# Later stores, later second row loads, an earlier gates' pool and a reordered last output in a graph layer of 32 batches

## The chip, the core and the metric

One Trainium2 chip, one core. Times are device microseconds of that core. A trace is one execution; a median is over 4 executions where no number is told.

## The reference, cut to what matters

```python
h = relu(layernorm(x))                              # x: (32, 512, 256) float32
# branch 1: convolution over the 512 positions
c = relu(bn1(conv1x1(h.T)));  c = bn2(conv17(c));  x_conv = relu(c + h.T).T
# branch 2: graph messages
s = h @ w_se.T + b_se                               # 3 features
A = exp(-|s_n - s_m|^2) * adj                       # (512, 512) for each batch
x_nmp = A @ relu(h @ w_msg.T + b_msg)
# gates
gi = [x_conv, x_nmp] @ w_ih.T + b_ih;  gh = h @ w_hh.T + b_hh
r = sigmoid(gi_r + gh_r);  z = sigmoid(gi_z + gh_z);  n = tanh(gi_n + r * gh_n)
out = x + (1 - z) * n + z * h
```

## The kernel before

TensorE does everything that is a product. The 17-tap convolution is 25 smaller products for each of seven groups of positions (175 in all), with additions on VectorE before (`x`, `xd`, `w`) and after (`z`, `y`). Five streams of work (rows, begins, graphs, conv, gates) are woven into one instruction order at build time: the program keeps a guessed clock `now` and guessed free times of VectorE and ScalarE, and each stream yields the time at which it may go on. Nothing of this is decided on the chip. There, each engine has its own list. In the trace before, a GpSimd store whose data was ready at 256.29 us left only at 260.12, behind a row's store for which GpSimd had stood 3.56 us.

A normalised and transposed row (512 KB) is `HT`. It is stored to DRAM (`hd`) and read back up to three times: as `hT` for the first convolution, as `hTg` for the messages, as `hTb` for the gates. The graph sums go out as `nd` and come back as `xnb`. The partial outputs of the convolution go out as `cd` and come back as `xconv`. GpSimd issues most stores, SyncE most loads.

```python
    def load_row(b):
        if b not in HR:
            HR[b] = front.tile([P, ND, N], F32, name="hT", bufs=2)
            nc.sync.dma_start(HR[b], HD[b])
            HR_AT[b] = now + 8.0

    def load_sums(b, d):                       # called behind the last product of gates(b - 1)
        if b < B and (b, d) not in XN:
            XN[b, d] = late.tile([P, N], F32, name="xnb", bufs=2)
            nc.sync.dma_start(XN[b, d], ND_[b, d])
# ... evacuate(): one partial output of the convolution
        part = late.tile([P, Q * U], F32, name="part", bufs=3)[:, : Q * (last - first)]
        act.activation(part..., y..., AF.Identity, bias=..., scale=...)
        act.free += 0.7
        PARTS.append(act.free + 4.0)           # the third next may not start before this
        later(act.free + 0.4, lambda: nc.gpsimd.dma_start(CD[b][:, o, n0:n1], part[:, : n1 - n0]))
# ... begin(b), the later rows (b >= 8): transposed by VectorE
            HT[b] = front.tile([P, ND, N], F32, name="hT", bufs=2)
            turning = True
            for o in range(ND):
                dve.transpose(HT[b][:, o, :], xb[:, o, :])
                if o < ND - 1:
                    yield dve.free
            nc.gpsimd.dma_start(HD[b], HT[b])
            begun, turning = b + 1, False
# ... all_rows()
                rows_wait = True
                for k in (b, b + 1):
                    if k in batches(g) and k < begun:
                        load_row(k)
                yield HR_AT[b]
                yield from rows(g, b)
# ... the convolution, from the 25th product on: a third weight is made from the two loaded
                if m == 24:
                    late_pools()               # loads whh and wih of the gates
                yield lambda: len(X2) > m and len(WS) > m
                if 25 <= m + 1 < 50 and W_AT[m + 1] <= now:
                    third_weight(m + 1)        # VectorE: w[:, 2] = w[:, 0] + w[:, 1]
# ... the streams: generator, guessed length, start
        "gates": (all_gates(), 31.25 * PER, 1.6),
```

## Time and profile before

| | us |
|---|---|
| time, median of 4 runs (range) | 2126.8 (2125.6 to 2129.2) |
| span of the profiled run | 2124.6 |
| TensorE busy | 2064.3 |
| of it lost to half clock | 21.1 |
| idle between the first and the last matmul | 49.4 |
| after the last matmul | 9.1 |

How to read it: busy, idle, 1.8 us of start-up and the end make the span. "Lost to half clock" is worked out: the busy time inside the trace's half-clock periods (granted clock 0.50 to 0.51), times one half. The lines behind these numbers stand in the prediction.

### The profile page before, as it was taken

To read this page: it belongs to the slowest core of one execution; us is meant where nothing else is said; L and a number is where in the kernel's file an instruction comes from. 1 tells how busy PE (TensorE), PEld (TensorE's weight loads), DVE (VectorE), ACT (ScalarE), POOL (GpSimd) and SP (SyncE) were. 2 spreads that over 40 slices of the span, in tenths; PEclk is the share of its full clock that TensorE was granted. 3 is DMA by queue.
4 is the path that set the end of the run, shared out by engine and by line. 5 is a ranking of instruction groups with operands and counts; after the bars stand their busy time and mean duration, and the time that the engine had idled before them with its cause. 6 is when DMAs were issued, how large, how long until landed. Compare 5 with 4: busy or idle time off the path is not lost. (4 is left out here: it accounts for less than half of the span.)

```text
span 2124.6 us, 25898 instructions
## 1 busy us (share of the span) xinstructions
PE 2064.3 (97%) x8756; PEld 1266.6 (60%) x8756; DVE 1511.3 (71%) x2660; ACT 756.9 (36%) x1267; POOL 339.9 (16%) x582
## 2 busy tenths in 40 slices
PE   9999899999999999999999999999999999999998
PEld 6887666655665555655566655556655566654443
DVE  6887779878874686875687857568876778863333
ACT  5555343235333235323353223443143522233111
POOL 2000212112111112110121111221111201112111
PEclk9999999999999999999999999999999999999999
DMA  7446778777766758676576775676876756624332
GB/s 282 169 145 205 248 240 217 199 205 208 215 180 200 188 140 226 186 204 188 152 218 177 198 203 164 181 190 192 224 193 168 203 165 161 171 57 134 85 93 40
DMA packets 546436, 383.07 MB, mean 180 GB/s; under 512 B 456576, under 2 KB 473472, under 8 KB 545664
## 3 DMA queue, kind: packets, MB, share of 16 engines
q1 hardware_dynamic: 512992, 282.17, 50.2%
q0 software_dynamic: 28624, 86.01, 11.8%
q10 hardware_dynamic: 4688, 13.24, 1.6%
q8 instruction: 70, 1.15, 0.2%
q14 instruction: 62, 0.51, 0.1%
HBM read 281.95 MB, written 99.35 MB: 179 GB/s over the span
## 5 line engine op out<-in xcount | busy, mean ns | idle before, releaser
L136 PE MATMUL ps_acc<-xnb,wih 128*128 128x512 f32 (+1 forms) x772 | 364.0, 594 | 2.5 <-DMA xnb<-nd 2.5
L136 PE MATMUL ps_acc<-xconv,wih 128*128 128x512 f32 (+1 forms) x772 | 363.2, 593 | 0.0
L136 PE MATMUL ps_acc<-hTb,whh 128*128 128x512 f32 x768 | 358.3, 596 | 4.5 <-DMA hTb<-hd 2.8
L136 PEld LDWEIGHTS ps_c<-xd,w 128*128 128x128 f32 x2400 | 294.0, 191 | 30.1 <-issue 24.7
L136 PE MATMUL ps_c<-xd,w 128*128 128x135 f32 (+1 forms) x2400 | 303.8, 279 | 1.0 <-DVE z L127 1.0
L1028 POOL DMA_DIRECT2D out_dram<-res x252 | 164.1, 657 | 610.7 <-DVE res L127 528.9
L136 PEld LDWEIGHTS ps_acc<-xnb,wih 128*128 128x128 f32 x772 | 143.5, 190 | 163.7 <-issue 154.7
L136 PEld LDWEIGHTS ps_acc<-xconv,wih 128*128 128x128 f32 x772 | 144.1, 191 | 158.2 <-issue 154.9
L136 PEld LDWEIGHTS ps_acc<-hTb,whh 128*128 128x128 f32 x768 | 141.7, 190 | 157.9 <-issue 147.2
L136 PE MATMUL ps_g<-at,msg 128*128 128x512 f32 x512 | 226.5, 593 | 0.6 <-DVE at L127 0.5
L136 PEld LDWEIGHTS ps_b<-x,w 128*128 128x128 f32 x1200 | 157.1, 191 | 50.9 <-issue 36.1
L136 PE MATMUL ps_b<-x,w 128*128 128x135 f32 (+1 forms) x1200 | 164.7, 280 | 8.1 <-ACT at L127 4.0
L127 DVE TENSOR_TENSOR r<-ps_acc,r 128x512 f32<-128x512 f32 (+1 forms) x65 | 44.3, 682 | 178.2 <-PE ps_acc L136 178.2
L127 ACT ACTIVATE mid<-ps_b 128x270 f32<-128x270 f32 (+1 forms) x150 | 59.5, 396 | 301.5 <-PE ps_b L136 293.8
L136 PEld LDWEIGHTS ps_g<-at,msg 128*128 128x128 f32 x512 | 95.8, 190 | 114.3 <-issue 111.5
L127 DVE TENSOR_TENSOR msg<-ps_g,bmsg 128x256 f32<-128x256 f32 x128 | 53.9, 422 | 137.6 <-PE ps_g L136 137.3
L136 PE MATMUL ps_g<-hT,w 128*128 128x512 f32 (+4 forms) x288 | 123.6, 579 | 23.2 <-DMA hT<-hd 23.2
L127 DVE SCALAR_TENSOR_TENSOR x<-x,x 128x544 f32<-128x544 f32 (+5 forms) x161 | 137.7, 855 | 2.7
L127 ACT ACTIVATE z<-ps_acc,brz 128x512 f32<-128x512 f32 x64 | 44.0, 687 | 248.5 <-PE ps_acc L136 235.3
L127 DVE TENSOR_TENSOR x<-x 128x272 f32<-128x272 f32 (+5 forms) x280 | 127.5, 500 | 0.3
L136 PE MATMUL ps_g<-wmsg,hTg 128*128 128x259 f32 x496 | 125.3, 384 | 0.3 <-DVE aug L127 0.3
L127 ACT ACTIVATE h<-ps_g,bn_shift,bn_scale 128x252 f32<-128x252 f32 (+4 forms) x208 | 85.4, 486 | 102.5 <-PE ps_g L136 101.9
(114 smaller groups left out, 2623.4 us busy)
## 6 DMA issues: line engine op xcount, KB each, us to landing
w<-wd SPq DMA_DIRECT2D x125, 768.0 KB, 5.4
m_sb<-in_adj_dram SPq DMA_DIRECT2D x384, 64.0 KB, 3.1
hd<-hT POOLq DMA_DIRECT2D x32, 512.0 KB, 6.0
hT<-hd SPq DMA_DIRECT2D x32, 512.0 KB, 4.2
hTb<-hd SPq DMA_DIRECT2D x32, 512.0 KB, 5.1
xnb<-nd SPq DMA_DIRECT2D x64, 256.0 KB, 3.2
xconv<-cd SPq DMA_DIRECT2D x32, 512.0 KB, 4.9
res<-in_x_dram SPq DMA_DIRECT2D x256, 64.0 KB, 2.8
```

The costliest lines, as they stand in the source:

```text
L127: getattr(self.engine, name)(*tiles, **more)
L136: nc.tensor.matmul(ps, lhsT, rhs, **more)
L1028: queue.dma_start(OB[b][:, s.start // 32 : s.stop // 32, o * P + 32 * g : o * P + 32 * g + 32], y[at, s].rearrange("i (k j) -> i k j", j=32),)
```

## The change

Its intent is to take waits from TensorE. It has six parts.

- **a, stores.** GpSimd's stores of rows and sums are put into its list when their data is expected, not at once, so that they don't hold up others.
- **b, rows.** A later row's store comes after both transposes; the second row is loaded 2.5 us after the first.
- **c, pool.** The gates' weights are loaded as soon as the 25 weights exist.
- **d, spacing.** Partial outputs 5 us apart instead of 4.
- **e, bank.** A product whose bank the exponentials hold is planned after them.
- **f, last output.** z times the old row is added before the last sum, the hidden state's product goes behind that of z, and the last sum is cut 384/128 instead of 256/256.

```diff
 # a
+    def store_at(t, dst, src):
+        todo = [lambda: nc.gpsimd.dma_start(dst, src)]
+        ...
+        STORES.append(run)
+        later(t, run)
+    def settle_stores():                       # called ahead of each new row tile and load
+        while STORES:
+            STORES.pop(0)()
-            nc.gpsimd.dma_start(HD[b], HT[b])
+            store_at(act.free + 0.4, HD[b], HT[b])
-        nc.gpsimd.dma_start(ND_[b, d], sums)
+        store_at(act.free + 0.4, ND_[b, d], sums)
 # b
             yield lambda: b not in NORMS
+            yield NORM_AT[b]
 ...
                 if o < ND - 1:
                     yield dve.free
+            yield dve.free + 0.4
             nc.gpsimd.dma_start(HD[b], HT[b])
 ...
-                for k in (b, b + 1):
-                    if k in batches(g) and k < begun:
-                        load_row(k)
+                load_row(b)
+                if b + 1 in batches(g) and b + 1 < begun:
+                    later(now + 2.5, lambda b=b: load_row(b + 1))
 # c
                 if m == 24:
+                    yield lambda: len(WS) >= 25
+                if late is None and len(WS) >= 25:
                     late_pools()
 # d
-        PARTS.append(act.free + 4.0)
+        PARTS.append(act.free + 5.0)
 # e
-                yield max(X_AT[m], W_AT[m])
+                yield max(X_AT[m], W_AT[m], bank_at if g > 0 else 0.0)
 # f
+            if is_last(o):
+                dve.tensor_tensor(z[:, s], z[:, s], r[:, s], op=ALU.mult)
+                dve.transpose(r[:, s], z[:, s])
+                dve.tensor_tensor(y[:, s], r[:, s], y[:, s], op=ALU.add)
 ...
+            dve.tensor_tensor(zh, z, hT[:, o, :], op=ALU.mult)            # mix_ahead
+            dve.tensor_scalar(z, z, -1.0, 1.0, op0=ALU.mult, op1=ALU.add)
+            dve.transpose(turned, zh)
+            dve.tensor_tensor(y, turned, y, op=ALU.add)
 ...
-            for h in range(2):
-                s = slice(h * N // 2, (h + 1) * N // 2)
+            for s in (slice(0, N - P), slice(N - P, N)):
```

More of the change, by code (lines that the diff above doesn't have):

```diff
@@ L164, in settle, with run @@
             LATER.pop(0)[1]()
+    STORES = []
+    def store_at(t, dst, src):
+        todo = [lambda: nc.gpsimd.dma_start(dst, src)]
+        def run():
+            if todo:
+                todo.pop()()
+        STORES.append(run)
[3 more added lines that the diff above has]
+            STORES.pop(0)()
     XS, HT, HB, HR, HR_AT, HG, XN, XR = {}, {}, {}, {}, {}, {}, {}, {}
@@ L191, in load_row @@
         if b not in HR:
+            settle_stores()
             HR[b] = front.tile([P, ND, N], F32, name="hT", bufs=2)
@@ L197, in load_graph @@
         if b < B and b not in HG and begun > b:
+            settle_stores()
             HG[b] = front.tile([P, ND, N], F32, name="hTg", bufs=1)
@@ L203, in load_gates @@
             return
+        settle_stores()
         HB[b] = late.tile([P, ND, N], F32, name="hTb", bufs=2)
@@ L228, in load_sums @@
         if b < B and (b, d) not in XN:
+            settle_stores()
             XN[b, d] = late.tile([P, N], F32, name="xnb", bufs=2)
@@ L367, in norm_t @@
         if d == 0:
+            settle_stores()
             HT[b] = front.tile([P, ND, N], F32, name="hT", bufs=2)
@@ L682 @@
     at_product = 0
-    freed, made, made_at = -1, 0, 0.0
+    freed, made, made_at, bank_at = -1, 0, 0.0, 0.0
     def all_operands():
@@ L826, in factors_t @@
     def factors_t():
+        settle_stores()
         ps = bank()
@@ L836, in kernel_exp @@
     def kernel_exp(at):
-        nonlocal now
+        nonlocal now, bank_at
         pss = [bps.tile([P, N], F32, name="ps_b"), bank(), bank(), bank()]
@@ L848, in kernel_exp @@
             act.activation(at[:, c, :], pss[c], AF.Exp)
+            if c == 0:
+                bank_at = act.free + LAG
     def masked(b, at, c):
@@ L905, in begin @@
             yield now + 8.0
+            settle_stores()
             HT[b] = front.tile([P, ND, N], F32, name="hT", bufs=2)
@@ L958, in graph @@
         yield act.free + LAG
+        settle_stores()
         at = front.tile([P, NT, N], F32, name="at", bufs=1)
@@ L979, in gates @@
         hT = HB[b]
-        parts = []
         x_in = []
@@ L1008, in mix_last, with leave, is_last, mix_ahead @@
         def mix_last(r, z, o, s):
-            if s.start == 0:
-                parts.append(late.tile([P, N], F32, name="o_sb"))
-            t = parts[-1]
-            dve.tensor_tensor(t[:, s], hT[:, o, s], r[:, s], op=ALU.subtract)
-            dve.tensor_tensor(t[:, s], z[:, s], t[:, s], op=ALU.mult)
-            dve.tensor_tensor(r[:, s], r[:, s], t[:, s], op=ALU.add)
-            later(dve.free, lambda: leave(r, t, o, s))
-        def leave(r, t, o, s):
-            dve.transpose(t[:, s], r[:, s])
-            y = XR[b, o]
-            dve.tensor_tensor(y[:, s], t[:, s], y[:, s], op=ALU.add)
-            later(dve.free + 0.4, lambda: store(y, o, s))
+            y = XR[b, o]
+            if is_last(o):
+                dve.tensor_tensor(z[:, s], z[:, s], r[:, s], op=ALU.mult)
+                dve.transpose(r[:, s], z[:, s])
+                dve.tensor_tensor(y[:, s], r[:, s], y[:, s], op=ALU.add)
+                later(dve.free + 0.4, lambda: store(y, o, s))
+                return
+            t = late.tile([P, N], F32, name="o_sb")
+            dve.tensor_tensor(t, hT[:, o, :], r, op=ALU.subtract)
+            dve.tensor_tensor(t, z, t, op=ALU.mult)
+            dve.tensor_tensor(r, r, t, op=ALU.add)
+            later(dve.free, lambda: leave(r, t, y, o))
+        def leave(r, t, y, o):
+            dve.transpose(t, r)
+            dve.tensor_tensor(y, t, y, op=ALU.add)
+            later(dve.free + 0.4, lambda: store(y, o, slice(0, N)))
+        def is_last(o):
+            return b == B - 1 and o == ND - 1
+        def mix_ahead(z, o):
+            y = XR[b, o]
+            zh, turned = (late.tile([P, Q * U], F32, name="part", bufs=3)[:, :N] for _ in range(2))
+            dve.tensor_tensor(zh, z, hT[:, o, :], op=ALU.mult)
+            dve.tensor_scalar(z, z, -1.0, 1.0, op0=ALU.mult, op1=ALU.add)
+            dve.transpose(turned, zh)
+            dve.tensor_tensor(y, turned, y, op=ALU.add)
         def store(y, o, s):
@@ L1044, in reset, with reset_hidden @@
                 act.activation(r, ps_r, AF.Sigmoid, bias=brz[:, o : o + 1])
-            def reset_hidden():
+            def reset_hidden(ps_h):
                 dve.scalar_tensor_tensor(
@@ L1085, in gates, with hidden @@
             yield from products(ps_r, o, 0, 1, 3, (0, 2), reset)
-            if ps_h is None:
-                ps_h = acc.tile([P, N], F32, name="ps_acc")
-                yield from products(ps_h, o, 2, 0, 1, (0, 0), reset_hidden)
-            else:
-                reset_hidden()
+            def hidden():
+                ps = acc.tile([P, N], F32, name="ps_acc")
+                yield from products(ps, o, 2, 0, 1, (0, 0), lambda: reset_hidden(ps))
+            if ps_h is not None:
+                reset_hidden(ps_h)
+            elif not is_last(o):
+                yield from hidden()
             ps_z = acc.tile([P, N], F32, name="ps_acc")
             yield from products(ps_z, o, 1, 0, 3, (0, 2), update)
+            if is_last(o):
+                later(act.free + 0.2, lambda: mix_ahead(z, o))
+                yield from hidden()
             if o == 0:
@@ L1101, in gates @@
                 continue
-            for h in range(2):
-                s = slice(h * N // 2, (h + 1) * N // 2)
-                if h > 0:
+            for s in (slice(0, N - P), slice(N - P, N)):
+                if s.start > 0:
                     ps_n = acc.tile([P, N], F32, name="ps_acc")
```

## The prediction

> **What bounds the kernel now.** I read the busy times of the page first, then TensorE's waits, then the same stretches in the timeline, then the stretches with their granted clock.
>
> The busy line names the engine:
> ```profile
> PE 2064.3 (97%) x8756; PEld 1266.6 (60%) x8756; DVE 1511.3 (71%) x2660; ACT 756.9 (36%) x1267; POOL 339.9 (16%) x582
> ```
> TensorE is busy for 2064.3 us of a span of 2124.6 us. So 60.3 us are idle, and nothing that the change does to another engine is worth anything unless it shortens these 60.3 us or makes the busy time itself shorter. Three stretches tell where the idle time lies (columns after the length: busy time and count for PE, PEld, DVE, ACT, POOL, then the granted clock, the DMA share and GB/s):
> ```profile
> 0.00:1899.00 1899.00, 1847.75 (x8244) 1169.49 (x8245) 1427.34 (x2544) 709.60 (x1207) 297.66 (x515) 0.99 0.67 191
> 1899.00:2115.60 216.60, 216.50 (x513) 97.09 (x511) 79.70 (x107) 46.74 (x59) 42.22 (x67) 1.00 0.35 89
> 2115.60:2124.50 8.90, 0.00 (x0) 0.00 (x0) 4.29 (x11) 0.51 (x1) 0.00 (x0) 0.69 0.18 30
> ```
> 51.3 us are idle before 1899 us, 0.1 us in the last 217 us of matmuls, and 8.9 us follow the last matmul. As the end of the matmul work is dense, any wait taken away earlier moves the end by as much. The table of TensorE's waits (us in total, times, longest) names the owners:
> ```profile
> PE ps_g L136 <- DMA hT<-hd: 23.2, 11, 4.3
> PE ps_b L842 <- ACT mid L127: 6.6, 1, 6.6
> PE ps_b L136 <- ACT at L127: 4.0, 5, 1.4
> PE ps_acc L136 <- DMA hTb<-hd: 2.8, 1, 2.8
> PE ps_b L136 <- ACT mid L127: 2.5, 1, 2.5
> PE ps_acc L136 <- DMA xnb<-nd: 2.5, 3, 1.2
> ```
> These six are 41.6 of the 51.3 us. The largest is the reload of a row of the normalised input (hT) from DRAM before the first convolution.
>
> **A second cost behind each wait.** Two equal groups of 16 matmul passes in the timeline:
> ```profile
> 429.35 8.80 PE L136 MATMUL ps_g<-hT,w 128*128 128x512 f32 x16 [3.83 <-DMA hT<-hd]
> ...
> 669.81 7.22 PE L136 MATMUL ps_g<-hT,w 128*128 128x512 f32 x16 [1.58 <-DMA hT<-hd]
> ```
> The first, after 3.83 us of idleness, took 1.6 us longer than the second, after 1.58 us. The granted clock says why:
> ```profile
> 429.30:432.80 3.50, 3.45 (x4) 0.51 0.82 294
> 433.00:436.40 3.40, 3.40 (x10) 1.00 0.19 29
> ```
> Half the clock for 3.4 us costs 1.7 us. Placing all half-clock periods of the trace beside the waits: those at 238, 266 to 276, 429, 481 to 487, 737, 996, 1406 to 1412 and 1723 us follow waits of 2.1 us or more; waits of 1.6 us or less had none. Leaving out the parts in which TensorE was idle anyway, they cost 1.7 + 3.1 + 1.7 + 2.7 + 1.7 + 1.7 + 3.4 + 1.7 = 17.7 us, inside "busy". Two more (30 and 190 us) follow no wait. So the waits are worth up to 51 + 18 us, not 51.
>
> [...] a row of 512 KB landed in 3.4 to 4.0 us alone (478.6, 732.6 us) and in 5.7 to 7.9 us beside a second row or a store (1244.1, 421.3 us). [...]
>
> **The change part by part.** I compared the instruction order of both builds. The matmul work is the same, instruction by instruction, but for the split of the last output; only the order moves. For distances below I add up the matmul work that stands between two instructions, with the trace's 0.43 us for a 512-wide pass (two passes to a product) and 0.115 us for a 135-wide one.
>
> *Stores of GpSimd, spacing of partial outputs, gates' pool sooner.* The worst single wait is at 262.8 to 269.4 us. The timeline of GpSimd there, then that of ScalarE (the bracket is the idle time before the instruction and what ended it):
> ```profile
> 255.49 0.54 POOL L674 DMA_DIRECT2D cd<-part  x1 [0.69 <-ACT part L127]
> 259.59 0.54 POOL L912 DMA_DIRECT2D hd<-hT  x1 [3.56 <-DVE aug L127]
> 260.12 0.54 POOL L674 DMA_DIRECT2D cd<-part  x1
> ```
> ```profile
> 267.19 1.35 ACT L127 ACTIVATE part<-y,bn_shift,bn_scale 128x522 f32<-128x522 f32 x1 [7.24 <-DMA cd<-part]
> ```
> And TensorE's own next line:
> ```profile
> 269.45 1.21 PE L842 MATMUL ps_b<-right,left 5*128 5x512 f32 x1 [6.62 <-ACT mid L127]
> ```
> The row's store, issued before its transposes were done, blocked GpSimd until 259.59; the partial outputs' stores behind it left 3 to 4 us late; ScalarE waited 7.24 us for a free buffer, and TensorE 6.62 us for ScalarE. In the new order three stores of partial outputs stand ahead of the row's store, the row's store comes after both transposes, and the fourth partial output comes some 8 us of matmul work after the first. So the 6.62 us and its 3.1 us of half clock should go. The gates' weights (whh, wih) are loaded 9.6 us of matmul work earlier and no longer just ahead of the hTb load, so the 2.75 us at 237.85 and 1.7 us of clock should go too. The other waits there (1.55, 0.78, 0.52) I leave. Of 14.2 us I count 13, as something always comes back.
>
> *Rows.* By row, wait before and what its new distance makes of it: 429 us: load to use 0 to 12 us, 3.8 goes; 482: store to use 2.6 to 6.9, 4.3 goes; 670: 1.6 goes (5.2 to 9.6); 737: 0 to 3.9, 3.6 goes; 996: 0 to 3.6, 2.4 goes; 1065: unchanged, 1.1 stays; 1250: loaded alone now, 2.4 becomes 1; 1263: 4.3 to 9.7, 1.4 goes; 1346: 0.3 goes; 1404: store to use falls from 7.4 to 4.0, so 2.1 becomes about 5.5. One row (b = 12, used near 465 us) falls from 8.2 to 0 us between load and use: about 2.5 new. 23.2 becomes 10.1: 13 us. Of its half clock (1.7 + 2.7 + 1.7 + 1.7 + 3.4 = 11.2 us), 3.4 stays and 1.7 comes new: 6 us. Together 19 us.
>
> *The bank of the exponentials.* Five products stood directly (0.6 us of work) behind the exponentials that free their bank and waited 4.0 us; three do now. 2 us.
>
> *The last output.* The trace of the end:
> ```profile
> 2115.53 0.42 DVE L127 TENSOR_TENSOR r<-ps_acc,r 128x256 f32<-128x256 f32 x1 [1.30 <-PE ps_acc L136]
> ...
> 2119.30 1.83 SPq L1028 DMA_DIRECT2D out_dram<-res  x4
> ...
> 2119.67 0.42 DVE L127 TENSOR_TENSOR res<-o_sb,res 128x256 f32<-128x256 f32 x1
> ```
> After the last product's addition at 2115.53 VectorE ran ten operations of 0.42 to 0.44 us, to 2120.1; the program ended 4.4 us later. Now six follow the last part's addition, per part one product, one transpose and one addition with the residual, because z times the old row is added before; the 384-wide ones cost about 0.55 us, the 128-wide ones about 0.28 us (estimates, from 0.69 us for 512 and 0.42 us for 256): 3 x 0.55 + 3 x 0.28 = 2.5 us against 4.1 us. But the tanh of the last part lies less well hidden, and the large stores hold 384 columns instead of 256. So I take 1.2 us of the 1.6 us.
>
> *New waits.* A new order meets new coincidences: sums loaded at their use (load to use under 5 us in 49 loads against 42) and operands a little later. I charge 4 us.
>
> Sum: 13 + 19 + 2 + 1.2 - 4 = 31 us, so 2127.9 - 31 = 2097 us.
>
> **Rivals.**
> A: *The waits only change places.* TensorE is 97% busy and the order is fixed at build time from the kernel's own guess of times; each row's wait may return at another row. For it: the count of rows with under 5 us between load and use falls only from 19 to 13 of 32. Against it: the biggest waits have named causes that the order removes. It would give 2112 to 2125 us.
> B: *Everything named goes, with its half clock.* It would give the six groups' 41.6 us, 17.7 us of clock and 1.2 us at the end: 60 us, about 2067. Against it: row 1404, whose distance gets shorter, and the 2.5 us wait at 1722.9, behind three long ScalarE copies that the change doesn't touch.
> C: *Loads collide more.* Loads moved later meet others[...]. That could eat 10 us: 2107.
> Slower than before would take over 30 us of new waits; nothing points there.
>
> **Range and chances.** 2097, with 2083 to 2113 for 8 in 10: the low end is three quarters of B, the high end is A with the early repair alone. Over 2% faster means 2085.3 or less, 43 us of at most 69: 0.13. Within 2%: 0.86. Slower: 0.01.
>
> **What would show it.** Right: TensorE's wait for hT at 7 to 14 us in total instead of 23.2; no 6.6 us wait for mid, no hTb wait; busy time down by 6 to 12 us, which only the clock can do, with the mean clock at about 0.99; the time from the last matmul to the end near 7.7 us. Wrong: waits for hT still above 18 us, a new wait over 4 us outside the rows, or busy time unchanged.

## The result, and the profile after

The changed kernel took 2114.7 us (median of 4 runs, 2112.7 to 2117.8) against 2126.8 us of the kernel before in the same rounds. The ratio is 0.9943, with a 95% interval of 0.9926 to 0.9960. All ratios here are the mean time of one kernel's runs over that of the other's runs of the same rounds, so not quite the ratio of the medians. Executions over 1.5% slower than the fastest of the same kernel are left out of the means. The output is correct, and it is 12 us faster where 31 us were predicted, outside the predicted range of 2083 to 2113.

The busy line of the page after:

```profile
PE 2062.1 (98%) x8756; PEld 1264.4 (60%) x8756; DVE 1513.1 (72%) x2660; ACT 759.9 (36%) x1267; POOL 337.4 (16%) x582
```

Busy time fell by 2.2 us where 6 to 12 were predicted, and the span by 10.6 us (2124.6 to 2114.0). TensorE's waits after (us in total, times, longest):

```profile
PE ps_acc L136 <- DMA xnb<-nd: 11.3, 6, 3.7
PE ps_g L136 <- DMA hT<-hd: 10.5, 5, 2.8
PE ps_b L136 <- DVE w L127: 3.4, 1, 3.4
PE ps_acc L136 <- ACT xconv L127: 2.6, 1, 2.6
...
PE ps_b L136 <- DVE x L127: 1.9, 1, 1.9
...
PE ps_b L136 <- ACT mid L127: 0.8, 1, 0.8
```

Beside the table before: the row's wait (hT) fell from 23.2 to 10.5 us, the 6.6 us for mid and the wait for hTb are gone. But the wait for the sums (xnb) rose from 2.5 to 11.3 us, two owners are new, xconv (2.6) and x (1.9), and w rose from 1.5 to 3.4. The stretches before and behind the dense end (length, then busy time and count of PE, PEld, DVE, ACT, POOL, then clock, DMA share, GB/s):

```profile
0.00:1888.00 1888.00, 1843.33 (x8239) 1166.81 (x8240) 1427.40 (x2542) 711.58 (x1206) 294.65 (x515) 0.99 0.68 192
...
2106.00:2114.00 8.00, 0.78 (x7) 0.59 (x6) 3.74 (x9) 0.91 (x2) 0.00 (x0) 0.71 0.20 33
```

44.7 us are idle before 1888 us, against 51.3 before; from the last matmul to the end it is 7.2 us against 9.1.

**Where the time went, in one ledger.** I added up all gaps in TensorE's records and the half-clock losses by stretch and by what ended the gap, in both traces:

| part of the sum | predicted | measured |
|---|---|---|
| start of the gates, 220 to 300 us: idle 12.2 to 13.1, half clock 4.9 to 3.4 | -13 | -0.5 |
| rows after 300 us: wait for hT 23.2 to 8.1 | -13 | -15.1 |
| rows: half clock behind these waits 11.1 to 1.7 | -6 | -9.4 |
| bank of the exponentials: 4.0 to 2.5 | -2 | -1.5 |
| last output: 9.06 to 7.20 | -1.2 | -1.9 |
| new waits: xnb after 300 us 2.5 to 11.3 (8.8), half clock behind them 4.9, half clock behind waits of 1.1 us or less 4.8 | +4 | +18.5 |
| rest (waits for mid after 300 us 2.5 to 1.3 and 1.7 us of half clock behind them, -2.9; small waits +1.4; other +0.7) | 0 | -0.8 |
| sum | -31 | -10.7 |

The spans differ by 10.6 us, so the ledger closes to 0.1 us. Two terms failed by 12.5 and 14.5 us; the rows gave 5.5 us more than was counted on. The rest of this document asks why the two failed, and how much of each number belongs to the change at all.

**The start of the gates.** TensorE's timeline after, with the idle time before each group in brackets:

```profile
230.92 3.93 PE L136 MATMUL ps_g<-hT,w 128*128 128x351 f32 x8 [2.43 <-DMA hT<-hd]
242.72 1.19 PE L136 MATMUL ps_b<-x,w 128*128 128x135 f32 x8 [1.95 <-DVE x L127]
...
271.31 1.19 PE L136 MATMUL ps_b<-x,w 128*128 128x135 f32 x8 [3.37 <-DVE w L127]
...
277.37 1.98 PE L136 MATMUL ps_acc<-xconv,wih 128*128 128x512 f32 x4 [2.60 <-ACT xconv L127]
```

Of these four owners only w had a wait in this stretch before, of 1.55 us. The third line is the clearest. It is the fourth product of the convolution's second group, and each product of that group needs one third weight, which VectorE adds up. In the trace before, the fourth product began at 261.74, and the fourth of these additions was this one:

```profile
257.59 0.69 DVE L127 TENSOR_TENSOR w<-w 128x512 f32<-128x512 f32 x1
```

It was done at 258.3, ahead of the 6.62 us wait (262.8 to 269.4) and not under its cover. After, the fourth addition comes 13 us later in time, behind two long additions:

```profile
266.27 1.85 DVE L127 TENSOR_TENSOR x<-h 128x1632 f32<-128x1632 f32 x1
268.16 1.86 DVE L127 SCALAR_TENSOR_TENSOR x<-x,x 128x1632 f32<-128x1632 f32 x1
...
270.57 0.68 DVE L127 TENSOR_TENSOR w<-w 128x512 f32<-128x512 f32 x1
```

The stretch 260 to 280 us before, then after, with the columns as above (third engine: VectorE):

```profile
260.00:280.00 20.00, 13.38 (x89) 11.68 (x89) 14.01 (x26) 9.20 (x14) 8.74 (x13) 0.74 0.83 282
```
```profile
260.00:280.00 20.00, 13.30 (x97) 10.64 (x96) 19.04 (x38) 13.35 (x20) 4.76 (x8) 1.00 0.92 315
```

VectorE rose from 14.0 to 19.0 of 20 us, and TensorE's busy time stayed at 13.3 us (at a mean clock of 1.00 instead of 0.74, so it did more). Over 220 to 300 us VectorE is busy for 60.3 us before and 61.1 us after, so its work has moved and hardly grown. So this wait for w was not hidden before: the new order made it. Which of the other new waits were hidden and which were made was not traced. ScalarE's own wait, which the change was to remove, became shorter but is still there, and the activation of xconv that TensorE waits for until 277.37 us stands behind it:

```profile
274.80 1.35 ACT L127 ACTIVATE part<-y,bn_shift,bn_scale 128x522 f32<-128x522 f32 x1 [4.93 <-DMA cd<-part]
```

It was 7.24 us. And GpSimd still holds stores up, here behind another instruction:

```profile
265.88 1.35 POOL L279 TENSOR_TENSOR rstd<-veps,mhalf 128x4 f32<-128x4 f32 x1 [6.92 <-DVE veps L127]
267.21 0.57 POOL L942 DMA_DIRECT2D hd<-hT  x1
267.77 0.54 POOL L696 DMA_DIRECT2D cd<-part  x1
```

A power for the normalisation was put into GpSimd's list before VectorE had its input ready, and GpSimd stood for 6.92 us. The partial output whose store comes behind it was itself done only at 265.50, so its store left 2.3 us late. The larger part is its landing: it left right behind the store of a row, and landed at 274.72, 6.95 us after its issue. Before it was the same: the store that ScalarE waited for was ready at 256.29, left behind a row's store at 260.12 (3.8 us late) and landed at 267.11, 6.99 us after its issue, while the partial output's store issued at 255.49 landed after 2.3 us. The prediction named the late issue only. That the row's store is what slows the landing no run tests.

**The sums.** Here is what SyncE issued at the first place, then TensorE's side of it:

```profile
732.51 0.33 SPq L211 DMA_DIRECT2D hT<-hd  x1
732.94 0.86 SPq L251 DMA_DIRECT2D xnb<-nd  x2
```
```profile
736.69 1.98 PE L136 MATMUL ps_acc<-xnb,wih 128*128 128x512 f32 x4 [1.72 <-DMA xnb<-nd]
```

In the trace before, TensorE waited 3.57 us at this place, at 736.66 us, for hT. The wait has only changed its owner: the row's load is held until the row's own store has landed (732.50), and the sums' load, next in the same list, leaves right behind it and lands at 736.64. At the costliest place SyncE's line and TensorE's are:

```profile
584.13 2.40 SPq L251 DMA_DIRECT2D xnb<-nd  x2
```
```profile
588.68 2.93 PE L136 MATMUL ps_acc<-xnb,wih 128*128 128x512 f32 x3 [3.73 <-DMA xnb<-nd]
```

TensorE was ready at 584.95 (588.68 - 3.73), 0.8 us after the load left; the first of the two issues alone took 1.92 us and landed 4.50 us after it began. At 510.7 us it is the same with 4.0 us of distance, an issue of 2.57 us and a landing of 6.90 us: 2.94 us. Both stand between loads of the adjacency; elsewhere the same issue took as little as 0.32 us. Over the whole trace the sums' loads (256 KB) landed 2.4 to 7.7 us after their issue began. The prediction had counted such short distances (49 loads under 5 us against 42) and charged too little for them.

### The profile page after: what moved, and what is told of

The parts are those of the page before. It is cut to its first block, busy times and chain, and to the rows that moved or that the text cites.

```text
span 2114.0 us, 25897 instructions
## 1 busy us (share of the span) xinstructions
PE 2062.1 (98%) x8756; PEld 1264.4 (60%) x8756; DVE 1513.1 (72%) x2660; ACT 759.9 (36%) x1267; POOL 337.4 (16%) x582
## 4 chain that ended last, share of the span: by engine, by line
PE 82%; DVE 5%; issue 5%; DMA 4%; ACT 2%; POOL 1%; SPq 0%; DVEq 0%; ACTq 0%; POOLq 0%
PE ps_acc L136 41%; PE ps_g L136 18%; PE ps_c L136 15%; PE ps_b L136 6%; DMA xnb<-nd 1%; PE ps_g L141 1%; PE ps_b L867 1%; DVE z L127 1%; DMA hT<-hd 1%; DVE at L127 1%; DMA hd<-hT 1%; DVE gg L127 1%; DVE x L127 1%; POOL out_dram L1074 0%; ACT y L127 0%
## 5 line engine op out<-in xcount | busy, mean ns | idle before, releaser
L136 PE MATMUL ps_acc<-xnb,wih 128*128 128x512 f32 (+1 forms) x772 | 366.1, 597 | 11.3 <-DMA xnb<-nd 11.3
L136 PE MATMUL ps_g<-hT,w 128*128 128x512 f32 (+4 forms) x288 | 119.3, 562 | 10.5 <-DMA hT<-hd 10.5
L127 DVE TENSOR_TENSOR xd<-x 128x544 f32<-128x544 f32 (+1 forms) x150 | 106.9, 719 | 23.8 <-PE ps_c L136 23.6
```

Source lines behind the costliest of these rows:

```text
L127: getattr(self.engine, name)(*tiles, **more)
L136: nc.tensor.matmul(ps, lhsT, rhs, **more)
```

## The experiments

Three theories, and the experiments are to part them.

1. *Stacked waits*: at the start the waits lie on top of each other; taking the top one away uncovers VectorE and ScalarE, so parts a, c and d are worth about nothing there.
2. *Given back*: parts a, c and d do their work, and the loss comes from what they do to the sums later.
3. *Order by chance*: any edit moves thousands of instructions in the woven order, and where loads then meet decides some 10 us either way, whatever the edit meant.

The quoted expectations were written before each run, each with its own rivals; its letters are its own. All kernels gave the right result. The kernel before was rerun in each batch: its medians were 2125.7, 2127.1, 2124.0, 2125.8 and 2125.2 us in the five batches (7, 7, 20, 10 and 7 runs), so kernels of different batches are comparable to some 3 us.

### First batch: one part alone

**tail_only**: part f on the kernel before.

```diff
-            for h in range(2):
-                s = slice(h * N // 2, (h + 1) * N // 2)
+            for s in (slice(0, N - P), slice(N - P, N)):   # with mix_ahead and is_last
```

> The kernel before with the last output's part of the change alone (its share of z made ahead, hidden product after z's, sum split 384/128). The instruction order is otherwise the same. Both theories: the time after the last matmul falls from 9.1 to about 7.2 us as in the changed kernel, so -1.9 us (ratio 0.9991), TensorE's other waits unchanged to 2 us in sum.

2126.3 us, ratio 1.0002 (0.9986 to 1.0018). The end after the last matmul fell from 9.06 to 7.97 us in its trace, too little to show in the time. This run taught something else. Its instruction order up to the last output is that of the kernel before, and its traced run lost 26.6 us to half clock against 21.1. The same eight products after the same wait, before, then here:

```profile
1156.93 1.19 PE L136 MATMUL ps_b<-x,w 128*128 128x135 f32 x8 [1.36 <-ACT at L127]
```
```profile
1158.45 2.10 PE L136 MATMUL ps_b<-x,w 128*128 128x135 f32 x8 [1.36 <-ACT at L127]
```

1.19 us at a granted clock of 1.00, 2.10 at 0.51. So a wait of 1.36 us may or may not be followed by half clock, in the same order of instructions. That is chance of the run, about 5 us of it, and the reason why medians are compared and not single traces.

**rows_only**: part b on the kernel before.

```diff
-                for k in (b, b + 1):
-                    if k in batches(g) and k < begun:
-                        load_row(k)
+                load_row(b)
+                if b + 1 in batches(g) and b + 1 < begun:
+                    later(now + 2.5, lambda b=b: load_row(b + 1))   # and the store after both transposes
```

> The kernel before with the rows' part alone: second row loaded 2.5 us later, a transposed row's store and its announcement only when the transposes are expected done. Theory 1 (a wait taken away is gone): waits for hT fall from 23 to about 10 us, other waits stay, half clock falls by 6 us, time -15 to -19 us. Theory 2 (the row's store still holds the same queue, so the wait moves to the next load behind it): hT falls to about 10, but waits for xnb or others rise by 6 us or more, time -3 to -9 us.

2110.4 us, ratio 0.9927 (0.9906 to 0.9947): 15 us faster, more than the whole change. Its waits:

```profile
PE ps_g L136 <- DMA hT<-hd: 8.1, 6, 2.4
PE ps_acc L136 <- DMA hTb<-hd: 5.7, 1, 5.7
```

hT fell from 23.2 to 8.1 us, xnb rose to 5.4 only. The 6.62 us wait for mid is gone here too, without parts a, c and d (it is part b that moves the row's store which blocked GpSimd), and what stands in its stretch is 13.3 us idle: hTb 5.7, w 3.4, hT 2.3.

**start_only**: parts a, c and d on the kernel before.

```diff
-            nc.gpsimd.dma_start(HD[b], HT[b])
+            store_at(act.free + 0.4, HD[b], HT[b])
-        PARTS.append(act.free + 4.0)
+        PARTS.append(act.free + 5.0)
+                if late is None and len(WS) >= 25:   # pool sooner
```

> The kernel before with the start's parts alone: GpSimd's stores when their data is expected, gates' pool laid out sooner, partial outputs spaced by 5.0 us. Theory 1 (prediction): the 6.6 us wait for mid and the 2.8 us wait for hTb go, idle time of TensorE between 220 and 300 us falls from 13 to about 4 us, time -10 to -13 us. Theory 2 (VectorE and the partial outputs' buffers bound this stretch once TensorE stops waiting): idle time there stays at 9 us or more under other names, time 0 +- 5 us.

2126.8 us, ratio 0.9994 (0.9977 to 1.0012): nothing. (Its profiled run was its fastest, 2120.9.) Its waits:

```profile
PE ps_g L136 <- DMA hT<-hd: 12.6, 7, 2.7
PE ps_acc L136 <- DMA xnb<-nd: 12.3, 5, 6.7
```

Two things follow. The 13 us of the prediction are not there, as theory 1 expects: the stretch 220 to 300 is 10.3 us idle against 12.2 and loses 3.2 us to half clock against 4.9, with w now waited for twice (5.1 us). And it swapped hT for xnb (hT down 10.6, xnb up 9.8 us), though of its parts only a touches the stores of rows and sums, and a alone does no such thing (stores_only below has hT at 19.8 and xnb at 3.2 us): that speaks for theory 2 or 3.

**jitter1**: nothing but a hair's shift of one planning constant in the kernel before.

```diff
-        "gates": (all_gates(), 31.25 * PER, 1.6),
+        "gates": (all_gates(), 31.25 * PER, 1.605),
```

> The kernel before with one constant of its own planning moved by a hair (the gates' starting place in the order, 1.6 to 1.605): no wait is aimed at, but the order of instructions shifts. Theory 1: same time within 3 us, the same waits at the same places. Theory 2 (where the waits fall is largely a matter of coincidence in the order): single waits of 2 us and more appear and vanish, hT and xnb waits change by 5 us or more each, time differs by 3 to 10 us either way.

2133.5 us, ratio 1.0030 (1.0013 to 1.0047): 7.8 us slower. The edit has no intent whatever. Its trace has hT at 25.3 and xnb at 7.5 us. So an effect of order alone reaches the size of what is to be explained.

### Second batch: what the parts are worth inside the change

**no_start**: the change without a, c and d.

```diff
-        PARTS.append(act.free + 5.0)
+        PARTS.append(act.free + 4.0)        # and stores and pool as before
```

> The changed kernel without its start parts (GpSimd's stores when expected, gates' pool sooner, partial outputs at 5.0 us): rows' part, bank and last output stay. If the parts add up, it is the rows' part's -15.3 us with 1 to 3 us more: about 2109 to 2111 us, 4 us faster than the changed kernel, which would make the start parts a loss there. If coincidence rules, anything within 8 us of the changed kernel's 2114.7, with other waits.

2106.7 us, ratio 0.9909 (0.9880 to 0.9937): 7 to 8 us better than the whole change. In its trace xnb is 5.8 us and the idle time after 300 us 17.9 against 26.2, while 220 to 300 us is as idle as ever, 12.9.

**stores_only**: part a on the kernel before.

```diff
-        nc.gpsimd.dma_start(ND_[b, d], sums)
+        store_at(act.free + 0.4, ND_[b, d], sums)   # and the rows' stores
```

> The kernel before with GpSimd's stores of rows and sums put where their data is expected, alone. Theory of the prediction: the partial outputs' stores no longer stand behind a waiting store, the 6.6 us wait for mid goes: -6 to -10 us. Rival: the row's store that blocked GpSimd there is that of a transposed row, which this part doesn't move, so the 6.6 us wait stays and the time is within 4 us of before.

2126.3 us, ratio 1.0001 (0.9977 to 1.0025). The 6.62 us wait stayed (6.5 us): moving these stores of GpSimd alone does not remove it.

**rows_reuse** and **after_reuse**: to test what a row's reading back costs, a row that was just transposed is used where it is. It is an edit beyond the change, on rows_only and on the changed kernel:

```diff
     def load_row(b):
+        if b not in HR and newest[0] == b:
+            HR[b], HR_AT[b] = HT[b], now        # still in its tile: no load
         if b not in HR:
+            newest[0] = -1                      # the next tile of this name takes its place
 ...
             HT[b] = front.tile([P, ND, N], F32, name="hT", bufs=2)
+            newest[0] = b
```

> The kernel before with the rows' part, and a row that was transposed just now is used from SBUF where it was made, not reloaded (9 of 32 reloads go, with their wait for the row's own store in SyncE's queue). If TensorE's waits for hT and for xnb behind it came from that queue: hT under 4 us, xnb under 4 us, half clock down by 3 us or more, 5 to 10 us faster than the rows' part alone (2100 to 2106). Rival (waits move on): within 4 us of 2110.4.

> The changed kernel with the same reuse of rows just transposed. Queue theory: xnb wait falls from 11.3 to under 7 us and hT from 10.5 to under 5 us, time 2103 to 2109. Rival: the three largest xnb waits (2.9, 3.7, 1.7 us) stand behind other loads and contention, so xnb stays near 10 us and the time near 2112.

rows_reuse 2099.9 us, ratio 0.9873 (0.9851 to 0.9895), 10.5 us under rows_only. after_reuse 2093.4 us, ratio 0.9839 (0.9814 to 0.9863), 21 us under the changed kernel. SyncE's waits for a row's store to land, in the changed kernel, then in after_reuse:

```profile
SPq L211 <- DMA hd<-hT: 61.7, 12, 8.8
```
```profile
SPq L216 <- DMA hd<-hT: 6.6, 2, 5.6
```

So 12 waits became 2, and 61.7 us became 6.6. hT falls from 10.5 to 4.4 us. But xnb stays at 9.8 us (against 11.3): so SyncE standing before a row's reload explains the sums' wait at 736.7 us, not the wait as a whole.

### Third batch: which of a, c and d, and how much is chance

**after_nopool**: the change without c. **after_nostores**: without a. **after_part4**: without d.

```diff
 # after_nopool
-                    yield lambda: len(WS) >= 25
-                if late is None and len(WS) >= 25:
                     late_pools()
 # after_nostores
-        store_at(act.free + 0.4, ND_[b, d], sums)
+        nc.gpsimd.dma_start(ND_[b, d], sums)        # and the rows' stores
 # after_part4
-        PARTS.append(act.free + 5.0)
+        PARTS.append(act.free + 4.0)
```

> The changed kernel with the gates' pool laid out as before. The order on VectorE and ScalarE is almost the changed kernel's (10 and 14 lines differ), so this shows the pool alone. If the pool sooner is worth what the prediction says: the wait for hTb returns (3 us with 1.7 us of half clock), time 3 to 5 us longer than the changed kernel. If the pool is what costs 8 us against the kernel without the start parts: 2106 to 2109.

> The changed kernel with GpSimd's stores of rows and sums placed as before. If these are the part that costs 8 us: 2106 to 2109 and xnb waits near 6 us. If the cost is a matter of the order as a whole: within 4 us of 2114.7 either way, xnb at 8 us or more.

> The changed kernel with partial outputs spaced by 4.0 us as before. If the spacing costs the 8 us: 2106 to 2109, xnb near 6 us. If the spacing is what keeps ScalarE from waiting for a buffer: a wait of ScalarE for the partial outputs' store of over 5 us near 270 us and TensorE's idle time between 220 and 300 us at 14 us or more.

after_nopool 2116.2 us (13 runs, 2109.2 to 2119.8), ratio 0.9963 (0.9952 to 0.9974): c is worth 1.5 us by the medians and 4 us by the ratios, no more than a hair's shift may do; without it the wait for hTb is back, 8.8 us. after_nostores 2114.6 us (7 runs), ratio 0.9956 (0.9941 to 0.9971): a is worth nothing that shows. after_part4 2101.3 us, ratio 0.9897 (0.9876 to 0.9917): d seemed to cost 13 us (10 us by the ratios), and xnb to fall with its removal from 11.3 to 5.9 us. That looked like the culprit of theory 2.

**after_jitter** is the changed kernel with the hair's shift, and in the fourth batch **part4_jitter** is after_part4 with it.

```diff
-        "gates": (all_gates(), 31.25 * PER, 1.6),
+        "gates": (all_gates(), 31.25 * PER, 1.605),
```

> The changed kernel with the gates' starting place in the planning moved by a hair (1.6 to 1.605), which aims at nothing. If the changed kernel's 8 us against the kernel without the start parts are a coincidence of its order: a difference of 3 to 10 us either way with xnb and hT waits at other places. If they belong to a part: within 3 us of 2114.7 with the same three large xnb waits.

> The changed kernel with partial outputs at 4.0 us, and the gates' starting place moved by a hair (1.605). If the 4.0 us spacing is itself worth 13 us against the changed kernel: within 3 us of 2101, against 2113 for the changed kernel with the same hair's shift. If the 13 us are a coincidence of the order between 515 and 750 us: no lasting gain, 2106 to 2116, with waits at other places.

after_jitter 2113.2 us (5 runs), ratio 0.9952 (0.9935 to 0.9969). part4_jitter 2115.9 us (6 runs), ratio 0.9953 (0.9936 to 0.9971). So with a hair's shift in both, the two spacings differ by 2.7 us in the medians and not at all in the ratios, which is within what batches differ by, and xnb is 10.4 us with the old spacing. The culprit falls: the 13 us belong to one order and not to the spacing as such.

### Fourth batch: buffers, the late weight, reuse once more

**after_xnb4**: four buffers for the sums instead of two; the adjacency's went from four to two to make room.

```diff
-            XN[b, d] = late.tile([P, N], F32, name="xnb", bufs=2)
+            XN[b, d] = late.tile([P, N], F32, name="xnb", bufs=4)
-                m = self.masks[b, c] = front.tile([P, N], F32, name="m_sb", bufs=4)
+                m = self.masks[b, c] = front.tile([P, N], F32, name="m_sb", bufs=2)
```

> The changed kernel in the same order of matmuls, with four buffers for the loaded sums (xnb) instead of two; the room comes from the adjacency rows, loaded two ahead instead of four. If a sums' load comes late because its buffer is freed only by the row before: the xnb wait falls from 11.3 to under 4 us and the half clock behind it (about 5 us) with it, time 2102 to 2108, unless waits for the adjacency rows appear. If it comes late for the queue in front of it or for traffic: xnb stays above 8 us.

2112.4 us (5 runs), ratio 0.9945 (0.9925 to 0.9964), and xnb 11.5 us. So it is not a buffer that the sums' loads wait for. (The adjacency with two buffers brought one new wait of 2.6 us.)

**after_third2**: the third weight is made two products ahead instead of one, which should take away the 3.4 us wait for w and nothing else.

```diff
-                if 25 <= m + 1 < 50 and W_AT[m + 1] <= now:
-                    third_weight(m + 1)
+                for k in (m + 1, m + 2):
+                    if 25 <= k < min(50, len(WS)) and W_AT[k] <= now:
+                        third_weight(k)
```

> The changed kernel with the third weights of the second group added up two products ahead instead of one. If the 3.4 us wait for VectorE's w near 271 us is only bad placing: it goes and TensorE's idle time between 220 and 300 us falls from 13.1 to below 10.5 us. If VectorE (19 of 20 us busy there) bounds the stretch: the idle time there stays at 12 us or more under other names (x, xd, at, xconv).

2090.9 us, ratio 0.9844 (0.9818 to 0.9869). The wait for w went, as meant. But the stretch 220 to 300 us stayed at 14.8 us idle (13.1 in the changed kernel), because the next one came up:

```profile
PE ps_g L141 <- ACT at L127: 5.9, 1, 5.9
```

That fits theory 1: taking one wait away doesn't shorten the stretch, and the one that comes up is again ScalarE's. Whether it was hidden before or made by this order isn't shown. With the reuse, which takes loads away, the stretch was shorter: 8.1 us idle in after_reuse. The 24 us were won elsewhere: idle time after 300 us fell from 26.2 to 10.2 us, and half clock there from 11.4 to 0, where the edit has no business at all.

**part4_reuse**: reuse on after_part4 (the same lines as after_reuse).

```diff
-        PARTS.append(act.free + 5.0)
+        PARTS.append(act.free + 4.0)            # and load_row with newest, as above
```

> The changed kernel with partial outputs at 4.0 us and rows just transposed used where they are. Additive: 2101 less the 10 to 20 us that the reuse gave twice, so 2081 to 2091 and faster than all others. Coincidence: within 5 us of the changed kernel with reuse alone (2093).

2095.5 us, ratio 0.9865 (0.9842 to 0.9888): 6 us under after_part4. Beside after_reuse (2093.4) it is also a third pair for the spacing. With the spacing of 5 us the sums' wait is longer in all three pairs (11.3 against 5.9, 11.6 against 10.4 with the hair's shift, 9.8 against 5.6 with the reuse), but the time is 13 us longer in one pair, and 2 to 3 us shorter in the other two, which is no more than batches differ by. Theory 2 holds that far: the spacing tends to bring the sums' waits, and other waits go in exchange.

### Fifth batch: is the best kernel lucky, and do the two gains add up

**third2_jitter** is after_third2 with the hair's shift; **third2_reuse** is after_third2 with the reuse.

```diff
 # third2_jitter
-        "gates": (all_gates(), 31.25 * PER, 1.6),
+        "gates": (all_gates(), 31.25 * PER, 1.605),
 # third2_reuse: load_row with newest, as above
```

> The kernel with the third-weight additions two products ahead, and the gates' planned start shifted by a hair (1.6 to 1.605). Theory A (the earlier addition is worth something by itself): 2088 to 2098 us, at least 15 us under the changed kernel with the same hair's shift (2113.2), and TensorE's wait for w in 260 to 280 us gone (under 1 us). Theory B (the 24 us were a lucky order): 2103 to 2116 us, the wait for w gone all the same, idle time after 300 us back at 17 us or more.

> Both together: third-weight additions two products ahead, and a row just transposed used in place instead of being read back. If the two gains stood for themselves (24 and 21 us) the time would be 2070 us; since they draw on the same idle time after 300 us (10.2 and 16.9 us left of 26.2) and on chance, I expect 2082 to 2094 us. TensorE's wait for hT 3 to 6 us.

third2_jitter 2107.0 us, ratio 0.9913 (0.9896 to 0.9929): in theory B's range, the wait for w gone all the same, with idle time after 300 us back at 20.8 us and hT and xnb at 8.6 and 9.3 us. So of the 24 us 6 by the medians (2113.2 to 2107.0) or 8 by the ratios remain with the shift in both, and the others went with the order. third2_reuse 2093.3 us, ratio 0.9842 (0.9827 to 0.9857): in its range of 2082 to 2094, at its upper end, and no gain over either edit alone. hT is 3.2 us, xnb 10.9.

**The hair's shift, side by side** (medians):

| kernel | constant 1.6 | constant 1.605 |
|---|---|---|
| before | 2125.7 | 2133.5 |
| changed kernel | 2114.7 | 2113.2 |
| changed, spacing 4 us | 2101.3 | 2115.9 |
| changed, third weight two ahead | 2090.9 | 2107.0 |

It moves a kernel by -1.4 to +16 us. Differences of under some 15 us between two such kernels, each tried in one order, don't tell what an edit is worth. What stands in spite of this is what repeats over orders. All fifteen kernels with part b are faster than the kernel before of their batch, by 8 to 35 us; none of the four without it is by more than 1 us (-1 to +8 us). And the reuse against the same kernel without it: -10.5, -21, -6 and +2 us, three of four down.

**Best version.** after_third2 (2090.9), third2_reuse (2093.3) and after_reuse (2093.4) beat both kernels by 21 to 24 and 32 to 35 us. The first is the fastest measured, by a lucky order; after_reuse removes a cost that its trace names, but was not tried with the hair's shift.

## Why the prediction was wrong

*The bound.* Right: TensorE's idle time and half clock are what can be won, and the last 217 us stayed dense.

*Stores, spacing, pool: 13 us.* This step failed. The prediction said "So the 6.62 us and its 3.1 us of half clock should go", and they went, as did the hTb wait. But it took the whole length of the waits as the gain, "as something always comes back" being given 1.2 us, and didn't ask when TensorE's other operands would be ready in the new order. They were late: hT, x, at, w and xconv cost 11.6 us in the same stretch, so that it is idle for 13.1 us after for 12.2 before, with half clock of 3.4 for 4.9. At least the wait for w was made by the new order: its addition, done at 258.3 before, was done at 271.25. start_only gave 0 us in time, and the change without these parts is 7 to 8 us faster than with them. GpSimd's blocked stores were rightly seen, but taking the wait away was not worth its length: stores_only leaves the wait, rows_only (with the row's store moved behind its transposes) removes it, and neither shortens the stretch (13.2 and 13.3 us idle).

*Rows: 19 us.* The mechanism was right, and the size too small. hT is 10.5 us in all where 10.1 were predicted; of these 2.4 us are a new one at 230.9, so after 300 us the fall was 15.1 us. Row by row it was not as told: 1404's row cost 2.8 us instead of 5.5, the one at 1250 2.3 instead of 1, the row of 482 us, whose wait was to go, still cost 1.4 us (now at 506 us), and the new wait near 465 us did not come: the row landed at 465.26 and was used at 465.30. The half clock behind the rows' waits fell by 9.4 us instead of 6. rows_only, with this part alone, is 15 us faster, in one order. One reading in support was off: the rows at 478.6 and 732.6 us (landed after 3.36 and 4.01 us) were not loaded "alone", since in both cases another load left 0.4 us behind them.

*Bank: 2 us, last output: 1.2 us.* Right in kind and size: 1.5 and 1.9 us in the trace. No run has the bank's part alone. In the time the last output can't be seen (tail_only). The tail of 7.7 us that was to show it came out at 7.2.

*New waits: 4 us.* This term was mis-sized, and it is the larger of the two failures: 18.5 us. The prediction had the mechanism, "sums loaded at their use", and counted seven more short distances, but charged 4 us for these and for late operands together. One such load costs 2.9 to 3.7 us when it stands 4.0 or 0.8 us before its use and lands after 6.9 or 4.5 us; two of these alone make 6.7 us. And it charged no half clock for them: 4.9 us behind the sums' waits. The other 4.8 us come from a rule that the prediction drew from one trace, "waits of 1.6 us or less had none". The changed kernel breaks it, with this line among others:

```profile
440.85 2.17 PE L136 MATMUL ps_b<-x,w 128*128 128x135 f32 x8 [0.79 <-ACT at L127]
```

Eight products took 2.17 us (granted clock 0.51 from 440.2 to 443.6 us), against 1.19 at a clock of 1.00, after waits of 0.29 and 0.79 us. Nor does a wait's length alone tell: in the trace before, the one of 2.41 us at 1249.85 us was followed by a clock of 1.00.

*The rivals.* A, that the waits only change places, came true, with its 2112 to 2125 us; it was given too little weight. Against it the prediction said that "the biggest waits have named causes that the order removes": they were removed, and others came, of the sums above all, which its count of rows could not show. C named collisions of loads; it was right in kind, as far as the landings of 4.50 and 6.90 us between other loads tell.

*What would show it.* Of the signs given, hT in 7 to 14 us, no mid and no hTb wait, a clock of 0.99 and the shorter end were all seen, and the time was still wrong. Busy time (down 2.2, not 6 to 12) was the sign that told it, and the new wait of over 4 us did not come: the sums' 11.3 us are six waits of up to 3.7 us.

*What stays open.* Why the sums' loads fall so near their use in some orders (9 to 12 us of waits in ten of the twenty kernels) and not in others (2 to 8 us in the other ten) is settled only so far: more buffers did not help (after_xnb4), the reload's wait on SyncE explains one place of six, the spacing of 5 us goes with the long waits in nine of ten kernels and that of 4 us in one of ten, and that one came by the hair's shift. By which steps the spacing moves the sums' loads no run shows. Of parts a, c and d only d was tried with a shifted order, and only with one shift. What brings half clock is open too. In the trace of the changed kernel it came with waits of 0.29 and 0.79 us (at 440 us, for 6.83 us at 0.50) and of 1.08 us (at 553 us, for 3.41 us at 0.50). Both times products that use 5 of 128 rows stand just ahead, as they do ahead of the two periods of the trace before at 30 and 190 us; whether they have to do with it was not tested.

## What to carry to other kernels

A wait's length, with the half clock behind it, is not yet what its removal gives (here 14.2 us were counted as 13, and start_only gave 0): before counting it, ask when each other input of the instructions behind it will be ready, in the new order and not only in the trace before, since a new order can make one of them late (here the addition of w, from 258.3 to 271.25 us). Where a scheduler fixes the order, shift one planning constant by a hair and time it before and after the change; an effect smaller than that shift's is not yet an effect. And where a load's distance to its use is counted, charge each short one with landing time less distance (here 4.50 less 0.8 and 6.90 less 4.0 us, for waits of 3.73 and 2.94 us), plus half clock (here 4.9 us behind the sums' waits), not with an average.
